# Two drains of TensorE in each group of four tiles of a graph layer

## The chip, the cores and the metric

The kernel runs on one core of a Trainium2 chip. Its time is the device time of one execution, in microseconds. A core has five engines with an instruction queue each: TensorE (PE; its weight loads are listed apart as PEld), VectorE (DVE), ScalarE (ACT), GpSimd (POOL) and SyncE (SP), which here issues transfers. Engines wait for each other through semaphores.

## The reference, cut to what matters

The reference is one layer of a graph network over 12500 nodes and 400000 edges with 128 features. Edges are sorted by `dst`; `src` is random. With `smu` a smooth bend (a linear part plus a Gelu-like part):

```
h   = max(layernorm(x), 0) @ W_in2f.T
Wij = (smu(edge_attr_20 @ W_f1.T + b_f1) @ W_f2.T + b_f2) * edge_weight[:, None]
agg = segment_sum(h[dst] * Wij, src, num_segments=12500)
out = x + smu(agg @ W_o1.T + b_o1) @ W_o2.T + b_o2
```

## The kernel before, in words

The 400000 edges are 3125 tiles of 128. Four tiles make a group (`GRP = 4`), two groups a super. A message of an edge is a row of 128 numbers. Since `src` is random, rows are first scattered by GpSimd into DRAM buffers, sorted by bins of 128 nodes; then the kept rows of a bin are fetched again and summed by TensorE with a one-hot matrix. The supers are cut into ten epochs (`PARTS`): while the rows of one epoch are made and scattered, the kept rows of the epoch before are summed. The first epoch has nothing to sum.

The order on TensorE, VectorE, ScalarE and SyncE is written out by hand (a manual schedule): each engine takes its instructions in the order in which the loop over `p`, the place of a group, names them. Semaphore waits are added where data or a buffer asks for them. In one turn the loop works on several groups at once. The steps, with the tile that each writes and its line:

- `turn` (L707): four transposes into `pt` on TensorE (L709, four matmuls, for the last epochs). `send` (L718 or L720, then four times L723): ScalarE scales `pt` into the message rows `ms`, and GpSimd scatters them (L738), four indirect transfers a group.
- `weigh` (L686): `pw`, an fp32 matmul of 128x512, from `sm`. `gather` (L667): `ph`, the rows of `h` by a one-hot matrix. `take` (L675): ScalarE copies `ph` into `hg`.
- `parts(...)`: sums of kept rows. It calls `add` (L799), fp32 matmuls of 128x128 into `pg`; about half of a turn's share stands here, the other half at the end of the turn. `add` also has VectorE make one-hot matrices (`se`, L783) and add a full `pg` to `agg` (L812), and has SyncE fetch the next rows (L769).
- `mix` (L696): VectorE, `mt` from `pw` and `hg`.
- `hide` (L633): `pu`, an fp32 matmul of 128x512. `bend` (L641): ScalarE, `ge` from `pu`. `smooth` (L649): VectorE, `sm` from `pu` and `ge`; the next turn's `weigh` reads it.
- `count` (L578, L580, L581): three small matmuls into `pc`, and `read` (L608), VectorE, `sl` from `pc`. `bins` (L564) and `pick_part` (L531, L532) make one-hot matrices for later groups.
- `step()`: in the first epoch, pieces of the preparation of `h` and of the indices.

`pu`, `pw`, `ph`, `pt` and `pc` have one PSUM bank each, `pg` has two. A tile is written again only when its readers are done. TensorE's order in a turn is so: `pt`, `pw`, `ph`, first half of the sums, `pu`, `pc`, second half of the sums.

```
            parts(lo + (hi - lo) // 2)
            mix(at(p + 1))
...
            read(at(p + 2))
            parts(hi)
            step()
```

Of the kernel before, what the change touches and what calls it, by code (L numbers as in the profile page):

```python
# [43 lines left out]
def gnn_kernel(  # L44
# [19 lines left out]
    nc = tc.nc  # L64
# [239 lines left out]
    with tc.tile_pool(name="ld", bufs=4) as ld, \  # L304
# [173 lines left out]
        def at(p):  # L478
            return seq[p] if p < len(seq) else NG

        def sup_at(p):
            return flow[p] if p < len(flow) else NS
# [5 lines left out]
        def load(s):  # L488
            if s >= NS:
                return  # L490
            t0, nt = sups[s]
            e0, n = t0 * P, nt * P
            fb = fbufs[place_of[s] % NF]
            if s > 0:
                nc.sync.dma_start(fb[0:R, :n], f_t[:, e0:e0 + n])
            loaded[s] = (fb,)
            if s > 2:
                targets(s)
# [112 lines left out]
        def number(g):  # L611
            if g >= NG:
                return
            (t, n), k = groups[g], epoch[g // PER]
            t0, hic = begins[k]
            if s_of(g) < EARLY:
                ix = cnt.tile([P, GRP], I32, name="ix", bufs=8)
            else:
                ix = ix_kept[:, t - kept_tile:t - kept_tile + n]
            nc.vector.scalar_tensor_tensor(ix[:, :n], slots.pop(g)[:, :n], BIG + CAP[k] - 1, hic[:, t - t0:t - t0 + n],  # L620
                                           op0=ALU.min, op1=ALU.add)
            taken[g] = ix
# [3 lines left out]
        def hide(g):  # L626

            if g >= NG:
                return
            n = groups[g][1] * P  # L630
            o = g % PER * GRP * P
            pu = ps1.tile([P, GRP * P], F32, name="pu")
            nc.tensor.matmul(pu[:, :n], w_f1, loaded[g // PER][0][:, o:o + n], start=True, stop=True)  # L633
            units_of[g] = pu
# [20 lines left out]
        def gather(g):  # L655

            if g >= NG:
                return
            n = groups[g][1] * P
            o = g % PER * GRP * P  # L660
            oh, hw = onehot[g // PER], loaded[g // PER][2]
            ph = ps1.tile([P, GRP * P], F32, name="ph")
            if g // PER < FEW // SUP:
                for q in range(3):
                    nc.tensor.matmul(ph[:, :n], hw[:, q * D:(q + 1) * D], oh[:, o:o + n], start=(q == 0), stop=(q == 2))
            else:
                nc.tensor.matmul(ph[:, :n], hw[:3 * WIN, g % PER, :], oh[:3 * WIN, o:o + n], start=True, stop=True)  # L667
            rows_of[g] = ph

        def take(g):  # L670
            if g >= NG:
                return
            n = groups[g][1] * P
            hg = edge.tile([P, GRP * P], F32, name="hg")
            nc.scalar.activation(hg[:, :n], rows_of[g][:, :n], AF.Copy)  # L675
            rows_of[g] = hg
# [3 lines left out]
        def weigh(g):  # L680

            if g >= NG:
                return
            n = groups[g][1] * P
            pw = ps1.tile([P, GRP * P], F32, name="pw")
            nc.tensor.matmul(pw[:, :n], w_f2, hidden.pop(g)[:, :n], start=True, stop=True)  # L686
            pws[g] = pw
# [3 lines left out]
        def mix(g):  # L691
            if g >= NG:
                return
            n = groups[g][1] * P
            mt = edge.tile([P, GRP * P], F32, name="mt", bufs=3)
            nc.vector.scalar_tensor_tensor(mt[:, :n], pws.pop(g)[:, :n], b2, rows_of.pop(g)[:, :n],  # L696
                                           op0=ALU.add, op1=ALU.mult)
            mixed[g] = mt

        def turn(g):  # L700

            n = groups[g][1]
            pt = ps1.tile([P, GRP, P], F32, name="pt")
            mt = mixed.pop(g)
            for j in range(n):
                if s_of(g) < EARLY:
                    nc.tensor.transpose(pt[:, j, :], mt[:, j * P:(j + 1) * P], ident)  # L707
                else:
                    nc.tensor.matmul(pt[:, j, :], mt[:, j * P:(j + 1) * P], w_o1, start=True, stop=True)  # L709
            mixed[g] = pt  # L710

        def send(g):

            t, n = groups[g]
            ms = msg.tile([P, GRP, ROW], F32, name="ms")
            m = epoch[s_of(g)] // BUFS
            if m:
                nc.scalar.activation(ms[:, :n, P], lo_b[:, t:t + n], AF.Identity, bias=mark[:, m:m + 1])  # L718
            else:
                nc.scalar.activation(ms[:, :n, P], lo_b[:, t:t + n], AF.Copy)  # L720
            pt = mixed.pop(g)
            for j in range(n):
                nc.scalar.activation(ms[:, j, 0:P], pt[:, j], AF.Copy, scale=w_sb[:, t + j:t + j + 1])  # L723
            if s_of(g) >= EARLY:
                nc.scalar.dma_start(kept_rows[:, t - kept_tile:t - kept_tile + n, :], ms[:, :n, :])
                return
            scatter(g, ms)
# [59 lines left out]
        def add(k, b, q):  # L787

            g = b % GRP
            c, i = b // SPAN[k], b % SPAN[k]  # L790
            halved = k == EPOCHS - 1 and b // GRP == whole // GRP - 1
            if halved:
                g %= GRP // 2
            if q == 0 and g == 0:
                pgs[0] = ps2.tile([P, GRP, P], F32, name="pg")
            if q == 0 and i == 0:
                choose(k, behind(k, c, 1))
            o = i * Q[k] + q
            nc.tensor.matmul(pgs[0][:, g, :], rows_in[c][:, o, 0:P], sel[c][:, o, :], start=(q == 0),  # L799
                             stop=(q == Q[k] - 1))  # L800
            if q < Q[k] - 1:
                return
            if i == SPAN[k] - 1 or b == NB - 1:
                rows_in.pop(c), sel.pop(c)
                fetch(k, behind(k, c, AHEAD))
            if g == GRP - 1 or b == NB - 1 or halved and g == GRP // 2 - 1:
                dst = agg[:, (b - g) * P:(b + 1) * P]
                src = pgs[0][:, :g + 1].rearrange("p b n -> p (b n)")
                if k == 0:
                    nc.vector.tensor_copy(dst, src)  # L810
                else:
                    nc.vector.tensor_add(dst, dst, src)  # L812
                if k == EPOCHS - SENT_LAST - 1:
                    plain.append(dst)
                    if len(plain) > 1:
                        fold()
# [20 lines left out]
        def parts(upto):  # L837
            nonlocal done
            while done < upto:
                add(summing, *work[done])  # L840
                done += 1
# [236 lines left out]
        def step():  # L1078

            nonlocal taken_steps, slot, apart_by  # L1080
            if opening:
                apart_by += 1
                if apart_by % 2 == 0:
                    opening.pop(0)()
                return
            slot += 1
            while taken_steps < COUNT and taken_steps * 3 * (eps_of[0][1] * PER - 22) < slot * COUNT:
                steps[taken_steps]()
                taken_steps += 1
# [49 lines left out]
        for p in range(len(seq)):  # L1139
            g = seq[p]  # L1140
            s = g // PER
            if p == (FEW // SUP - 3) * PER:
                assert not opening
            if p % PER == 0:
                load(sup_at(p // PER + 3))
            if s < EARLY:
                k = chores(g)
            else:
                lo = hi = done
            if p > 1 and p != SLACK:  # L1150
                turn(at(p - (p > SLACK)))
                send(at(p - (p > SLACK)))
            step()
            number(at(p + 1))
            weigh(at(p + 1))
            gather(at(p + 1))
            take(at(p + 1))
            parts(lo + (hi - lo) // 2)
            mix(at(p + 1))
            if p == 0:  # L1160
                turn(at(1))
                send(at(1))
                pick_part(at(2))
            step()
            hide(at(p + 2))
            bend(at(p + 2))
            count(at(p + 2))
            smooth(at(p + 2))
            pick_part(at(p + 3))
            bins(at(p + 3))  # L1170
            read(at(p + 2))
            parts(hi)
            step()
            assert k == 0 or taken_steps == COUNT

# [281 lines left out]
```

## Time and profile before

| | |
|---|---|
| median of 3 runs | 5191.76 us (5183.92 to 5208.39) |
| profiled execution | 5192.84 us |
| its span | 5190.7 us, 69995 instructions |
| TensorE busy | 3896.6 us (75%) |
| VectorE, ScalarE, GpSimd busy | 3349.5 (65%), 2957.4 (57%), 3042.1 us (59%) |
| mean granted clock of TensorE | 0.887 |

How to read the profile. A group's row gives the source line, engine, operation, what is written and read, the count, then the busy time in us, the mean of one in ns, the idle time of the engine just before, and what ended most of that. The chain of waits is followed back from the last instruction, at each step to what released it, or to the instruction before it on its engine; "issue" in it is time in which the engine waited for nothing that the profile shows. In a list of waits stand the waiter, what ended the wait, the total in us, the number of times and the longest. In a timeline stand start and duration in us, with the idle time before in brackets. The ends of matmuls are modelled: they say when the last result should be out, and the next matmul may start before that. In the source view of a line the durations are in ns, as least, median and greatest.

### The profile page before, as it was taken

Reading aid. Unit: us, or ns where it says so; the run is one execution under the profiler, and the core shown is the slowest. Engines: PE = TensorE matmul, PEld = TensorE weight load, DVE = VectorE, ACT = ScalarE, POOL = GpSimd, SP = SyncE. Lnnn points to the kernel's source line nnn. Section 1 sums busy time; section 2 is a strip of 40 time slices with the busy share of each in tenths; the row PEclk is TensorE's granted clock in tenths of the full one; section 3 lists DMA queues with packets and bytes.
Section 4 is the critical chain, followed back from the end, with each engine's and each line's share of the span. In section 5 each row is a group of like instructions: output and inputs, shape, how many; then the busy total and the mean of one; then the engine's idle time right before and its main releaser. Section 6 shows DMA issues by size and latency. Waiting matters only on the chain.

```text
span 5190.7 us, 69995 instructions
## 1 busy us (share of the span) xinstructions
PE 3896.6 (75%) x18475; PEld 2442.9 (47%) x18475; DVE 3349.5 (65%) x7364; ACT 2957.4 (57%) x7286; POOL 3042.1 (59%) x3170
## 2 busy tenths in 40 slices
PE   7667767777777777777777777777778877777456
PEld 3233334444444444444444444545455555545446
DVE  6675656666666666666666666666667767667236
ACT  6567866666565565666566666655556655555001
POOL 5666665555555555555565555555656665555554
PEclk9888888988898989989898989999989999989678
DMA  5644434544444443343444344444444444444566
GB/s 158 169 138 139 141 112 147 145 146 145 139 133 122 117 118 116 118 119 115 116 125 117 118 118 131 128 129 127 124 131 145 143 128 147 140 122 147 191 195 199
DMA packets 509824, 708.03 MB, mean 136 GB/s; under 512 B 174382, under 2 KB 362815, under 8 KB 509289
## 3 DMA queue, kind: packets, MB, share of 16 engines
q1 hardware_dynamic: 401992, 484.14, 33.2%
q0 software_dynamic: 100112, 207.06, 12.1%
q10 hardware_dynamic: 7312, 12.29, 0.6%
q8 instruction: 147, 2.41, 0.2%
q14 instruction: 261, 2.13, 0.2%
HBM read 409.48 MB, written 293.71 MB: 135 GB/s over the span
## 4 chain that ended last, share of the span: by engine, by line
PE 49%; DVE 17%; ACT 12%; issue 11%; another core or an unknown queue 10%; DMA 1%; ACTq 0%; POOL 0%; DVEq 0%; POOLq 0%
PE pw L686 14%; PE pg L799 13%; PE pu L633 10%; ACT ms L723 5%; DVE mt L696 5%; DVE sm L649 4%; PE ph L667 3%; DVE se L783 3%; PE pt L707 3%; ACT hg L675 3%; ACT ge L641 2%; DVE so L564 2%; PE pc L581 1%; PE pc L578 1%
## 5 line engine op out<-in xcount | busy, mean ns | idle before, releaser
L738 POOL DMA_INDIRECT buf<-ms,ix x2944 | 2826.0, 960 | 1974.5 <-ACT ms L723 1196.9
L686 PE MATMUL pw<-sm,w_f 128*128 128x512 f32 x1562 | 1024.6, 742 | 771.9 <-DVE sm L649 479.1
L799 PEld LDWEIGHTS pg<-se,rw 128*128 128x128 f32 x8036 | 1153.0, 207 | 450.6 <-issue 372.6
L799 PE MATMUL pg<-se,rw 128*128 128x128 f32 x8036 | 1245.6, 295 | 134.1 <-issue 101.3
L723 ACT ACTIVATE ms<-pt,w_sb 128x128 f32<-128x128 f32 x3121 | 879.5, 363 | 816.5 <-PE pc L581 294.4
L696 DVE SCALAR_TENSOR_TENSOR mt<-pw,b,hg 128x512 f32<-128x512 f32 x781 | 584.0, 748 | 790.5 <-ACT hg L675 585.8
L564 DVE SCALAR_TENSOR_TENSOR so<-irow_ps,hi_f,so 128x98 f16<-128x98 f32 x2936 | 931.4, 317 | 80.3 <-DVE so L564 2.3
L633 PE MATMUL pu<-f,w_f 128*128 128x512 f32 x1562 | 904.6, 664 | 0.0
L641 ACT ACTIVATE ge<-pu 128x512 f32<-128x512 f32 x781 | 472.2, 605 | 740.3 <-remote 224.0
L649 DVE SCALAR_TENSOR_TENSOR sm<-pu,ge 128x512 f32<-128x512 f32 x781 | 535.0, 685 | 477.0 <-ACT ge L641 269.3
L686 PEld LDWEIGHTS pw<-sm,w_f 128*128 128x128 f32 x1562 | 261.2, 210 | 926.6 <-DVE sm L649 553.0
L707 PE MATMUL pt<-ident,mt 128*128 128x128 f32 x2940 | 468.0, 283 | 266.6 <-ACT ms L723 208.7
L675 ACT ACTIVATE hg<-ph 128x512 f32<-128x512 f32 x781 | 472.6, 605 | 289.5 <-PE ph L667 85.2
L783 DVE TENSOR_TENSOR se<-irow_ps,rw 128x1536 f32<-128x1536 f32 (+1 forms) x345 | 587.9, 1704 | 71.9 <-remote 28.3
L532 ACT ACTIVATE oh<-oh,onesb 128x512 bf16<-128x512 bf16 x780 | 562.6, 721 | 26.2 <-ACT oh L531 0.9
L531 ACT ACTIVATE oh<-rbc,nrow 128x512 bf16<-128x512 uint8 x762 | 553.3, 726 | 0.0
L707 PEld LDWEIGHTS pt<-ident,mt 128*128 128x128 f32 x2940 | 341.8, 145 | 312.9 <-ACT ms L723 243.2
L608 DVE TENSOR_REDUCE sl<-pc 128x4 f32<-128x392 f32 x782 | 435.5, 557 | 67.1 <-PE ph L667 22.9
L667 PE MATMUL ph<-oh,hw 126*128 126x512 bf16 x762 | 337.7, 443 | 0.0
L633 PEld LDWEIGHTS pu<-f,w_f 128*128 128x128 f32 x1562 | 292.2, 221 | 81.3 <-issue 66.1
L812 DVE TENSOR_TENSOR agg<-agg,pg 128x512 f32<-128x512 f32 (+1 forms) x200 | 134.4, 672 | 281.2 <-remote 178.1
L578 PE MATMUL pc<-so,tri 128*128 128x392 f16 x736 | 254.4, 346 | 20.6 <-DVE sl L608 13.6
(218 smaller groups left out, 2120.6 us busy)
## 6 DMA issues: line engine op xcount, KB each, us to landing
rw<-buf SPq DMA_DIRECT2D x292, 774.0 KB
buf<-zero SPq DMA_DIRECT2D x146, 387.0 KB
rbc<-rel_dram SPq DMA_DIRECT2D x389, 128.0 KB
buf<-ms,ix POOLq DMA_INDIRECT x2944
rw<-buf SPq DMA_DIRECT2D x49, 645.0 KB
f<-in_f_t SPq DMA_DIRECT2D x390, 80.0 KB
hw<-h_dram SPq DMA_DIRECT2D x762, 31.5 KB
kept_rows<-ms ACTq DMA_DIRECT2D x45, 258.0 KB
```

The source lines that it names most:

```text
L564: nc.vector.scalar_tensor_tensor(so[:, j], irow_ps[:, :NB], hi_f[:, t + j:t + j + 1], so[:, j - 1] if j else before, op0=ALU.is_equal, op1 ...
L633: nc.tensor.matmul(pu[:, :n], w_f1, loaded[g // PER][0][:, o:o + n], start=True, stop=True)
L641: nc.scalar.activation(ge[:, :n], units_of[g][:, :n], AF.Gelu, scale=ZS)
L649: nc.vector.scalar_tensor_tensor(sm[:, :n], units_of.pop(g)[:, :n], LIN, hidden[g][:, :n], op0=ALU.mult, op1=ALU.add)
L675: nc.scalar.activation(hg[:, :n], rows_of[g][:, :n], AF.Copy)
L686: nc.tensor.matmul(pw[:, :n], w_f2, hidden.pop(g)[:, :n], start=True, stop=True)
L696: nc.vector.scalar_tensor_tensor(mt[:, :n], pws.pop(g)[:, :n], b2, rows_of.pop(g)[:, :n], op0=ALU.add, op1=ALU.mult)
L707: nc.tensor.transpose(pt[:, j, :], mt[:, j * P:(j + 1) * P], ident)
L723: nc.scalar.activation(ms[:, j, 0:P], pt[:, j], AF.Copy, scale=w_sb[:, t + j:t + j + 1])
L738: i = nc.gpsimd.indirect_dma_start(out=bufs[k][:, :], out_offset=bass.IndirectOffsetOnAxis(ap=ix[:, j:j + 1], axis=0), in_=ms[:, j, :], in ...
L783: nc.vector.tensor_tensor(se[:, a:a + n], own.unsqueeze(1).to_broadcast([P, n, P]), rows_in[c][:, a:a + n, P:P + 1].to_broadcast([P, n, P] ...
L799: nc.tensor.matmul(pgs[0][:, g, :], rows_in[c][:, o, 0:P], sel[c][:, o, :], start=(q == 0), stop=(q == Q[k] - 1))
```

## The change

A call is added in two places of the loop. It puts a drain instruction into TensorE's queue, which is to hold back what follows on TensorE until what stands ahead of it there is done. The first stands behind the first half of the sums (`mix` in between is VectorE's), ahead of `hide`. The second stands behind the second half of the sums, ahead of the next turn's `turn` and `weigh`. There are 782 turns, so 1564 drains. Nothing else in the order of any engine is changed.

```
--- before.py
+++ after.py
@@ -1157,6 +1157,7 @@
             take(at(p + 1))
             parts(lo + (hi - lo) // 2)
             mix(at(p + 1))
+            nc.tensor.drain()
             if p == 0:
                 turn(at(1))
                 send(at(1))
@@ -1170,6 +1171,7 @@
             bins(at(p + 3))
             read(at(p + 2))
             parts(hi)
+            nc.tensor.drain()
             step()
             assert k == 0 or taken_steps == COUNT
 
```

More of the change, by code (lines that the diff above doesn't have):

```diff
@@ L1159, in gnn_kernel @@
             mix(at(p + 1))
+            nc.tensor.drain()
             if p == 0:
@@ L1172, in gnn_kernel @@
             parts(hi)
+            nc.tensor.drain()
             step()
```

## The prediction

> **What bounds the kernel now.** I read the page first, then the chain of waits, then the waits of TensorE, then a timeline of some groups. The page gives the span, TensorE's busy share and the chain by engine; the chain's own view gives finer shares by line.
>
> ```profile
> span 5190.7 us, 69995 instructions
> PE 49%; DVE 17%; ACT 12%; issue 11%; another core or an unknown queue 10%; DMA 1%; ACTq 0%; POOL 0%; DVEq 0%; POOLq 0%
> L686 PE MATMUL pw<-sm,w_f 128*128 128x512 f32 x1562 | 1024.6, 742 | 771.9 <-DVE sm L649 479.1
> ...
> L633 PE MATMUL pu<-f,w_f 128*128 128x512 f32 x1562 | 904.6, 664 | 0.0
> ```
> ```profile
> core 0: 5190.7 us, clock 0.887
> ```
> ```profile
> by line: PE pw L686 14.3%; PE pg L799 12.9%; issue 11.4%; another core or an unknown queue 9.6%; PE pu L633 9.6%; ACT ms L723 4.8%; DVE mt L696 4.6%; DVE sm L649 3.9%; PE ph L667 3.4%; DVE se L783 3.1%; PE pt L707 2.7%; ACT hg L675 2.5%; AC
> ```
>
> Half of the chain runs through TensorE, but no engine is full: `pw` alone sees 771.9 us of idle TensorE before it. An fp32 matmul leaves two records, so x1562 is 781 groups of four tiles, some 6 us each; the 782 turns of the loop hold 1564 drains. How the chain goes through a group shows in the chain between 2404 and 2413 us:
>
> ```profile
> 2404.44 2.68 issue
> 2407.12 1.12 PE pw L686 x2
> 2408.24 0.22 PE ph L667
> 2408.46 0.45 PE pg L799 x4
> 2408.91 0.86 PE pu L633 x2
> ...
> 2410.11 0.74 PE pg L799 x6
> 2410.84 0.44 PE pt L707 x4
> 2411.28 0.49 issue
> 2411.77 1.14 PE pw L686 x2
> ```
>
> Reader: one turn of TensorE, from `pw` over the first half of the sums (`pg`), `pu`, the second half, `pt`, back to `pw`, is 4.16 us of work (2407.12 to 2411.28) in 4.65 us. The first drain stands between the first `pg` and `pu`, the second between the second `pg` and `pt`. While the chain runs on TensorE its pieces follow each other without a hole, since a matmul starts before the one ahead has ended. Where TensorE waits, it is nearly always at these two places:
>
> ```profile
> PE pw L686 <- DVE sm L649: 479.1, 269, 7.8
> PE pt L707 <- ACT ms L723: 208.7, 147, 3.5
> PE pw L686 <- issue: 182.8, 152, 5.5
> ...
> PE pw L686 <- DVE mt L696: 81.7, 73, 2.6
> ...
> PE pt L707 <- DVE mt L696: 32.4, 13, 8.4
> ...
> PE pt L707 <- issue: 20.8, 18, 6.3
> ```
>
> So `pw` waits in 494 of 781 groups, and the true loop is `pu` -> ScalarE's `ge` -> VectorE's `sm` -> the next `pw`. `pu` lies on that loop; `pt` mostly does not.
>
> **What one drain costs.** Nothing is removed or moved; each drain adds a wait, for TensorE's own earlier work. Queued behind the first are `pu`, the three counts `pc` and the second half of the sums; ScalarE's `ge` and VectorE's `sl` wait for these. Queued behind the second are `pt`, `pw` and `ph`; ScalarE's `ms` and `hg` and VectorE's `mt` wait for them, and SyncE's fetch of the next rows for the sums. In the first part of the run there are no sums yet, and the drains stand behind `ph` and `pc`.
>
> The trace has no drain behind matmuls, so the price comes from both sides. The cheap end is the drain records themselves, at the program's end:
>
> ```profile
> L1453 POOLq DRAIN  x3: 40/113/4402, 5180.7 to 5190.4; - x3
> ...
> L1453 PEldq DRAIN  x2: 8/8/8, 5187.9 to 5190.2; - x2
> ```
>
> TensorE's took 8 ns with nothing ahead of them, and one of GpSimd's stood 4402 ns, so a drain can stand long. The other end is a restart after a wait, next to a matmul in the stream:
>
> ```profile
> 2416.39 0.69 DVE L649 SCALAR_TENSOR_TENSOR sm<-pu,ge 128x512 f32<-128x512 f32 x1
> 2417.13 1.12 PE L686 MATMUL pw<-sm,w_f 128*128 128x512 f32 x2 [1.20 <-DVE mt L696]
> 2418.09 0.38 PE L667 MATMUL ph<-oh,hw 126*128 126x512 bf16 x1
> 2418.75 1.02 PE L633 MATMUL pu<-f,w_f 128*128 128x512 f32 x2
> ```
>
> `sm` ends at 2417.08 and `pw` starts at 2417.13: 0.05 to 0.06 us of restart. From idle the pair takes 1.12 us on the chain, in the stream an equal pair (`pu`) advances it by 0.86: 0.26 us, since its weights are then loaded in the open and the overlap with the matmul ahead (`pw` ends at 2418.25, `ph` starts at 2418.09) is gone. I take 0.26 + 0.06 = 0.32 us for a drain that waits for the array, because a drain makes exactly the state that `pw` starts from.
>
> The Trainium skill, PSUM — Partial Sum Buffer, section Engine vs sequencer instructions, says that a drain waits for the engine to go fully idle; by that the 8 ns are no price, and GpSimd's 4402 ns agrees. Its page TensorE: Matmul & The Clock Gate, section Single matmul latency, puts the part of a matmul that is hidden in a stream at 398 cycles of 2.4 GHz, an estimate of 0.17 us a drain; the trace shows an overlap of 0.16 us, and by that alone the sum below would be about half.
>
> **The sum.** First drain: `pu` has 9.6% of the span on the chain, 498 us. One pass is 0.86 us at full clock, 0.97 at the mean clock of 0.887, so some 514 groups have it on the chain: 514 x 0.32 = 164 us. In the other groups `ge` is held by something later and the drain is hidden. Second drain: in the 494 groups in which `pw` waits, `pw` still comes when `sm` does, and the drain vanishes there. Of the 287 others, `pt` itself already waits in 178 of 781 groups (23%), for ScalarE, and a drain costs nothing beside that wait: 222 groups x 0.32 = 71 us. I take half, 35 us, by judgement: in the chain above `pt` is followed both times by an issue piece, not by `pw`. Together 199 us. The profiled execution took 5192.84 us (span 5190.7 and 2.1 around it), the median of the runs is 5191.76; so **5192.84 + 199 = 5392 us**. Own range of this case: 5275 (0.16 us, the lost overlap alone, at the 514 first drains) to 5520 (both drains on the path in two groups of three, 781 x 2/3 x 0.64 = 333 us).
>
> **Rivals.** One thing in the trace makes a drain's price uncertain: signals of TensorE that arrive late.
>
> ```profile
> 2415.33 0.60 PE L707 MATMUL pt<-ident,mt 128*128 128x128 f32 x4
> ...
> 2416.32 0.29 ACT L718 ACTIVATE ms<-lo_b,mark 128x4 f32<-128x4 bf16 x1
> ...
> 2420.86 1.14 ACT L723 ACTIVATE ms<-pt,w_sb 128x128 f32<-128x128 f32 x4 [4.25 <-PE pc L581]
> ...
> 2422.35 0.62 ACT L641 ACTIVATE ge<-pu 128x512 f32<-128x512 f32 x1
> ...
> 2423.92 0.70 PE L686 MATMUL pw<-sm,w_f 128*128 128x512 f32 x1 [1.21 <-DVE mt L696]
> ```
> ```profile
>   PE pc L581: 294.4, 92
>   remote: 241.4, 68
>   PE pg L799: 120.3, 39
>   PE pu L633: 76.0, 32
>   PE ph L667: 66.7, 44
>   PE pt L707: 6.9, 13
> ```
>
> `ms` reads only `pt`, which ended at 2415.93, yet starts 4.9 us later. By the source view of L723 (second fence) this is common: 798.8 us of ScalarE's idle time in 275 cases, 2.9 us each, end at other matmuls' signals or at none that is known, and only 6.9 us at `pt`. Something holds TensorE's signals back while its matmuls go on.
>
> 1. *The drain waits for held signals too* (slower still). Then TensorE, which now runs ahead during a hold, stands to its end. In the case shown this would be free: with `pu` restarted at 2420.9 it ends by 2422.0, before `ge` at 2422.35, and the rest, 0.34 of counts (2409.77 to 2410.11 in the chain above), 0.74 of sums, 0.32 and 0.44 of `pt`, by 2423.9, when `pw` starts at 2423.92. It costs where a held signal has no reader waiting; no view counts those. With half as many as the seen ones, 138, at 2.9 us less the mean idle before `pw` (771.9 / 781 = 1.0 us), it is 262 us more: 5654; with as many, 5915. For it: 4402 ns of GpSimd's drain.
> 2. *Faster.* If a full TensorE queue is what holds the signals, emptying it twice a group lets `ms`, and so `hg` and `mt`, go sooner. With half of the 798.8 us taken as on the path, it wins if more than 199 / 400, one half, of the holds go; with three quarters gone, 5192.84 + 199 - 300 = 5092. Against it: holds outlast an idle TensorE, as here, where TensorE had stood idle for 2.1 of its 3.31 us when the late `ms` began:
>
> ```profile
> 2432.19 1.14 ACT L723 ACTIVATE ms<-pt,w_sb 128x128 f32<-128x128 f32 x4 [3.88 <-remote]
> 2433.39 2.08 PE L709 MATMUL pt<-w_o,mt 128*128 128x128 f32 x8 [3.31 <-ACT ms L723]
> ```
>
> 3. *The drain does nothing*: it only passes TensorE's sequencer, at 8 ns. 1564 x 0.008 = 12.5 us, all on the path: 5205, no change that can be told.
>
> **How the numbers follow.** The runs before lie within 0.5% of each other, so 0.5% (26 us) is about what can be told from no change. Forecast as summed: 0.43. Held signals: 0.34. No effect: 0.10. Faster: 0.13. So faster 0.13, same 0.10, slower 0.77. The range reaches down to 5150, which leaves out about two thirds of the faster case (0.09), and up to 5780, which leaves out the upper third of the held-signal case (0.10). The likeliest case alone is 5275 to 5520.
>
> **What would show it.** Right: `pu` loses its overlap with the sums, its idle time before rises from 0 to 0.2 us or more in nearly every group, and its mean grows from 664 ns towards the 742 of `pw`; `pt` gains idle time that is put down to no engine; `pw` waits less. Held signals: drain records on TensorE of 1 us and more, and `pu` idle by over 1 us a group. Faster: ScalarE's idle time before L723 falls by more than half. No effect: `pu` still starts before the last `pg` ends (its idle time before is 0.0 us in its row above). My forecast is wrong if the time is under 5218 us, or if `pu`'s idle time is there and the span does not grow by half of it.

## The result, and the profile after

The changed kernel takes 5917.48 us (median of 6 runs, 5893.33 to 5975.86), the kernel before 5210.66 us in the same set (6 runs, 5183.92 to 5230.16). The ratio is 1.1374, with an interval of 1.1314 to 1.1434: slower, and beyond the predicted range, which ended at 5780. It lies 2.5 us from the upper figure of the first rival, "with as many, 5915". The profiled execution took 5923.98 us, 731 more than that of before.

For what follows one thing must be known: the kernel before took about 5200 us in some sets of runs and 4037 us in others, each set on one chip and steady in itself, so every difference in time below is taken inside its own set, unless it is said that two sets are compared.

The page of the changed kernel: the span, TensorE's busy time, the chain by engine, and the groups of `pu`, `ge`, `pw` and `pt` (busy us, mean ns | idle us before).

```profile
span 5921.8 us, 71559 instructions
...
PE 4258.6 (72%) x18475; PEld 2605.8 (44%) x18475; DVE 3367.3 (57%) x7364; ACT 2999.2 (51%) x7286; POOL 3041.4 (51%) x3170
...
PE 60%; issue 25%; ACT 7%; DVE 4%; another core or an unknown queue 3%; DMA 1%; SPq 0%; ACTq 0%; DVEq 0%
...
L633 PE MATMUL pu<-f,w_f 128*128 128x512 f32 x1562 | 1062.1, 767 | 1004.7 <-issue 949.3
...
L641 ACT ACTIVATE ge<-pu 128x512 f32<-128x512 f32 x781 | 466.9, 598 | 1709.7 <-PE pu L633 1365.5
...
L686 PE MATMUL pw<-sm,w_f 128*128 128x512 f32 x1562 | 907.4, 665 | 71.0 <-DVE sm L649 39.4
...
L707 PE MATMUL pt<-ident,mt 128*128 128x128 f32 x2940 | 541.3, 313 | 305.8 <-issue 221.0
```

The idle time of TensorE has changed places: `pu` had 0.0 and has 1004.7 us, `pw` had 771.9 and has 71.0. In all TensorE is busy for 362 us more (4258.6 against 3896.6) and idle for 369 us more (5921.8 - 4258.6 = 1663.2, against 5190.7 - 3896.6 = 1294.1); together 731, the whole difference. In the chain, "issue", waits for nothing that the profile shows, grew from 11% to 25%.

The waits of TensorE in the changed kernel (waiter, what ended the wait, us in total, times, longest):

```profile
PE pu L633 <- issue: 949.3, 273, 8.1
PE pt L707 <- issue: 221.0, 95, 5.6
...
PE pt L709 <- issue: 43.4, 12, 5.0
PE pw L686 <- DVE sm L649: 39.4, 54, 2.6
```

These are not 781 small restarts but 273 + 95 + 12 = 380 long stops, 1213.7 us in all, 3.2 us each on the mean, nearly all of them behind the two drains (`pt` had 18 waits of this kind before, 20.8 us). The source views of the drains themselves and of L723 (durations in ns as least, median, greatest; then who ended ScalarE's idle time, in us and times):

```profile
L1160 PEldq DRAIN  x782: 593/2651/9807, 17.2 to 5525.9; - x196
```
```profile
L1174 PEldq DRAIN  x782: 1157/2373/7612, 20.5 to 5527.8; - x196
```
```profile
  PE pt L707: 383.0, 282
...
  remote: 30.4, 11
```

Before, `ms` (L723) waited for signals that were named after matmuls behind `pt` (294.4 us at `pc`, 241.4 unknown, 120.3 at `pg`), and 6.9 us at `pt`. Now it is `pt` itself, since TensorE can no longer run ahead of a late signal. The timeline shows one such stop, at the second drain (start, duration, idle before in brackets):

```profile
2697.45 0.21 PE L581 MATMUL pc<-so,rest_h 128*128 128x98 f16 x1
...
2701.93 0.57 DVE L608 TENSOR_REDUCE sl<-pc 128x4 f32<-128x392 f32 x1 [1.70 <-remote]
...
2702.66 2.07 PE L709 MATMUL pt<-w_o,mt 128*128 128x128 f32 x8 [5.00 <-issue]
2704.52 1.91 PE L686 MATMUL pw<-sm,w_f 128*128 128x512 f32 x2
...
2708.79 1.15 PE L709 MATMUL pt<-w_o,mt 128*128 128x128 f32 x8
...
2709.78 1.10 PE L686 MATMUL pw<-sm,w_f 128*128 128x512 f32 x2
```

The last count ends at 2697.66, and TensorE has nothing in flight. VectorE's `sl`, which reads that count, starts only at 2701.93, 4.3 us later. The drain lets `pt` go at 2702.66, 5.0 us after the array's last work. So the drain did not wait for the array; it let go only after the late signal had gone out.

One stop is one case. The trace also records the updates of semaphores, which are the signals themselves. It has 393 idle times of TensorE of over 0.5 us that end with a drain. In 277 of them a signal of TensorE goes out more than 0.15 us after the array fell idle, and from the last such signal to TensorE's next matmul it is 0.14 us at the median. (In the others none is recorded, but about a quarter of TensorE's updates are missing from this trace; the last section comes back to this.) In the trace of the same kernel without late signals (both_again, below) none of TensorE's 106 idle times of that length ends with a drain, and none has a signal inside. That the drain waits for the signals is the plain reading; that both wait for a third thing, these records do not exclude.

There is a second bill: `pt` then takes 2.07 us where the next one takes 1.15, and `pw` 1.91 where the next takes 1.10. The windows behind the stop and one turn later (us, busy time of the engines, then the granted clock) say why:

```profile
2702.70:2708.20 5.50, 5.39 (x14) 2.92 (x15) 0.68 (x1) 1.74 (x5) 0.00 (x0) 0.56 0.13 49
2708.70:2713.00 4.30, 4.10 (x21) 2.65 (x21) 2.80 (x8) 3.61 (x10) 0.00 (x0) 1.00 0.12 16
```

The granted clock is 0.56 in the 5.5 us behind the stop and 1.00 after that. The Trainium skill, TensorE: Matmul & The Clock Gate, section What's actually happening, has the array fall to half its clock after an idle window of about 3.4 us and come back after a busy one of the same length. The trace's records of the clock put the half from 2700.70 to 2707.53 us: the fall, 3.0 us after the last count's end, agrees, while the full clock came back 4.9 us after TensorE had started again, later than that.

A turn without a late signal shows the plain price of a drain, in the chain of the changed kernel:

```profile
2711.55 0.11 issue
2711.66 1.12 PE pu L633 x2
...
2713.85 0.08 issue
2713.93 0.65 PE pt L707 x4
```

`pu` costs 0.11 + 1.12 where it cost 0.86, so 0.37 us; `pt` 0.08 + 0.65 where it cost 0.44, so 0.29 us. The predicted 0.32 lies between them.

### The profile page after: what moved, and what is told of

The parts are those of the page before. It is cut to its first block, busy times and chain, and to the rows that moved or that the text cites. A ratio compares the mean times of both kernels' runs of the same rounds, so it can differ in the third digit from the quotient of the medians.

```text
span 5921.8 us, 71559 instructions
## 1 busy us (share of the span) xinstructions
PE 4258.6 (72%) x18475; PEld 2605.8 (44%) x18475; DVE 3367.3 (57%) x7364; ACT 2999.2 (51%) x7286; POOL 3041.4 (51%) x3170
## 4 chain that ended last, share of the span: by engine, by line
PE 60%; issue 25%; ACT 7%; DVE 4%; another core or an unknown queue 3%; DMA 1%; SPq 0%; ACTq 0%; DVEq 0%
PE pg L799 16%; PE pu L633 16%; PE pw L686 12%; PE pt L707 8%; PE ph L667 3%; PE pc L578 2%; ACT ge L641 2%; ACT oh L531 2%; PE pc L580 1%; ACT ms L723 1%; DVE se L783 1%; PE pt L709 1%; DVE sm L649 1%; DVE mt L696 1%
## 5 line engine op out<-in xcount | busy, mean ns | idle before, releaser
L738 POOL DMA_INDIRECT buf<-ms,ix x2944 | 2825.4, 960 | 2705.0 <-ACT ms L723 1908.4
L633 PE MATMUL pu<-f,w_f 128*128 128x512 f32 x1562 | 1062.1, 767 | 1004.7 <-issue 949.3
L799 PE MATMUL pg<-se,rw 128*128 128x128 f32 x8036 | 1325.6, 309 | 101.3 <-issue 83.3
L799 PEld LDWEIGHTS pg<-se,rw 128*128 128x128 f32 x8036 | 1221.4, 219 | 384.9 <-issue 315.8
L723 ACT ACTIVATE ms<-pt,w_sb 128x128 f32<-128x128 f32 x3121 | 881.0, 364 | 529.0 <-PE pt L707 383.0
L686 PE MATMUL pw<-sm,w_f 128*128 128x512 f32 x1562 | 907.4, 665 | 71.0 <-DVE sm L649 39.4
L633 PEld LDWEIGHTS pu<-f,w_f 128*128 128x128 f32 x1562 | 274.1, 220 | 1257.5 <-issue 1236.4
L707 PE MATMUL pt<-ident,mt 128*128 128x128 f32 x2940 | 541.3, 313 | 305.8 <-issue 221.0
L667 PE MATMUL ph<-oh,hw 126*128 126x512 bf16 x762 | 311.0, 408 | 0.0
L578 PE MATMUL pc<-so,tri 128*128 128x392 f16 x736 | 280.3, 381 | 0.2 <-DVE so L564 0.2
```

Source lines behind the costliest of these rows:

```text
L738: i = nc.gpsimd.indirect_dma_start(out=bufs[k][:, :], out_offset=bass.IndirectOffsetOnAxis(ap=ix[:, j:j + 1], axis=0), in_=ms[:, j, :], in ...
```

## The experiments

Two theories were to be told apart. **H**: a drain waits for signals of TensorE that come late, and the 707 us (5917.48 - 5210.66) are mostly those stops. **R**: the drains cost their restarts, 0.3 us each where they lie on the path, and nothing else. The kernel before was run beside all of them. Times are medians in us, each beside the median of the kernel before in the same set:

| kernel | drains | before | time | difference | ratio |
|---|---|---|---|---|---|
| d1_only | first place alone | 4037.09 | 4080.31 | +43 | 1.0107 (1.009 to 1.0123) |
| d2_only | second place alone | 4037.09 | 4035.53 | -2 | 0.9999 (0.999 to 1.0009) |
| ns_before | none, no scatter | 4037.09 | 3807.61 | -229 | 0.9433 (0.9418 to 0.9449) |
| ns_after | both, no scatter | 4037.09 | 3995.14 | -42 | 0.9898 (0.9882 to 0.9915) |
| both_again | both | 4035.28 | 4100.21 | +65 | 1.016 (1.0143 to 1.0177) |
| four_each | four at each place | 4035.28 | 4350.15 | +315 | 1.0782 (1.0764 to 1.08) |
| both_third | both | 4036.34 | 4101.47 | +65 | 1.0161 (1.014 to 1.0181) |
| ns_after2 | both, no scatter | 4036.34 | 3994.25 | -42 | 0.9895 (0.9875 to 0.9915) |
| drain_at_pw | one, between `pt` and `pw` | 4036.34 | 4037.11 | +1 | 1.0002 (0.9992 to 1.0011) |
| ahead_of_sums | both, each ahead of its half of the sums | 4044.78 | 4116.24 | +71 | 1.0177 (1.016 to 1.0194) |
| ns_before2 | none, no scatter | 4044.78 | 3806.21 | -239 | 0.941 (0.9391 to 0.9429) |
| first_epoch | both, first epoch only | 5288.05 | 5307.20 | +19 | 1.0039 (1.0002 to 1.0076) |
| both_hold | both | 5179.48 | 5928.63 | +749 | 1.1444 (1.136 to 1.1528) |
| d1_hold | first place alone | 5179.48 | 5615.51 | +436 | 1.084 (1.0759 to 1.0921) |
| d2_hold | second place alone | 5179.48 | 5473.99 | +295 | 1.0563 (1.0486 to 1.064) |
| pw_hold | one, between `pt` and `pw` | 5179.48 | 5413.26 | +234 | 1.0429 (1.0337 to 1.0521) |

before_again (the kernel before, 4036.85) and ns_after3 (no scatter, both drains, 3996.98, beside a kernel before of 5288.05) have one time each and no interval.

**One place at a time, d1_only and d2_only.** Each keeps one of the two calls:

```
             mix(at(p + 1))
+            nc.tensor.drain()        (d1_only)
...
             parts(hi)
+            nc.tensor.drain()        (d2_only)
```

> Only the first drain of each turn is kept (behind the first half of the sums, ahead of pu). Theory H (a drain waits until TensorE's signals are out, and these are held back for microseconds at a time): a hold is met by whichever drain comes first in it, so one drain alone meets most holds and the two single costs sum to more than the 727 us of both: here 450 to 600 us over before, about 5650 to 5800, and idle time before pu of 800 to 1000 us. Theory R (a drain costs its restart, and nothing else): the chain of the changed kernel gives 1.23 us for drain, restart and pu in place of 0.86, so 0.37 x 782 = 289 us at most, and the costs of the two add up to the whole.

> Only the second drain of each turn is kept (behind the second half of the sums, ahead of pt). Theory H: 300 to 500 us over before, about 5500 to 5700, with idle time before pt well above the 266.6 us of before, and this plus the first drain's own cost above 727 us. Theory R: 0.29 x 782 = 227 us at most, and it adds up with the first to 727 us or less.

The first drain alone cost 43 us and the second nothing. But the kernel before stood at 4037 us here, not 5200, so neither theory was tested by this set: whatever is late in the result's profile was not there.

**Without the scatter, ns_before and ns_after.** GpSimd's scatter (L738) returns before it issues, and the buffers are cleared whole, so kept rows are sums of zeros; TensorE, VectorE and ScalarE keep their instructions.

```
-    CB = 2
+    CB = 1
...
+                return               (ahead of L738)
```

> The kernel before with GpSimd's indirect transfers of the message rows (L738) left out; the buffers are cleared whole in their place, so that the sums read zeros. The output is not the reference's. Theory H, with the scatter as what holds TensorE's signals: the idle time of ScalarE before L723 that ends at other matmuls' signals than pt's falls from 799 us to under 150, and the time falls to 4000 to 4500 us. If the scatter does not hold them, that idle time stays above 500 us.

> The changed kernel with the scatter left out in the same way; the output is not the reference's. Theory H with the scatter as the holder: both drains cost their restart alone, at most 0.37 + 0.29 us a turn, 516 us, and less where TensorE waits anyway: 150 to 450 us over the same kernel without drains, and no drain record much above 4 us. Theory R: the same 600 to 800 us as with the scatter, or more, since TensorE then sets the pace alone. If the holds have another cause, the long drains (up to 9.8 us) stay.

Nothing was late in this set even with the scatter, so the pair does not yet tell whether the scatter holds the signals; the 4000 to 4500 us expected of ns_before were missed for the same reason. The pair does give a price of restarts: the drains cost 3995.14 - 3807.61 = 188 us here, near the 199 of the prediction's sum. The pages say where that holds, in ns_before and in ns_after:

```profile
PE 3421.0 (90%) x18470; PEld 2229.7 (59%) x18475; DVE 3318.4 (87%) x7364; ACT 2955.7 (78%) x7286; POOL 41.4 (1%) x45
```
```profile
PE 3684.7 (92%) x18470; PEld 2265.5 (57%) x18475; DVE 3333.7 (84%) x7364; ACT 2948.6 (74%) x7286; POOL 41.4 (1%) x45
```

TensorE is busy for 90% of that span, and the scatter, whose transfers make most of the 14% that DMA holds in the chain of the kernel before at this speed (before_again, below), is gone. It fits that fewer restarts find cover then; no run varies this alone. ns_after2 and ns_before2 repeat the pair in two other sets and give the same times within 2 us.

> The changed kernel without the scatter (part of the computation is left out), once more. If before takes about 4037 us: 3995 as before. If before takes some 5200 us: theory H with the scatter as the holder says under 4300 us and no drain above 6 us; if something else holds the signals, the time stays above 4600 us.

> The kernel before without the scatter (part of the computation is left out), once more. If before takes about 4037 us: 3808 again. If it takes some 5200 us: the scatter as the holder says under 4200 us, and ScalarE's idle time before L723 under 150 us; something else as the holder says over 4600 us.

**The changed kernel and the kernel before again, both_again and before_again.** Both are unchanged copies.

> The changed kernel once more, beside a kernel before that may take 4037 us, as in the last set, or some 5200, as in the first. Theory H (the 727 us come from TensorE's signals held back): where before takes about 4037 us and ScalarE's idle time before L723 ends at pt alone, both drains cost about their two single costs, 43 and 0 us, and at most the 188 us that they cost without the scatter: 4080 to 4220 us. Where before takes about 5200, the ratio is 1.13 again. Theory R (restart, whatever the signals do): 1.10 to 1.14 in both.

> The kernel before, for its profile in this set. Theory H: if it takes about 4037 us, the list of what ends ScalarE's idle time before L723 holds pt alone (under 20 us in all, in place of 799 us at other signals), and SyncE's register moves (L519, up to 1395 ns in the first set) all take under 60 ns; if it takes about 5200, both are as in the first set. Rival: the 1150 us between the sets are the granted clock or the transfers alone, and the odd idle time before L723 is in both.

This set too had its kernel before at 4035 us, and the change cost 65 us. before_again shows what is missing at that speed: in the source view of L723 nothing is late, in that of SyncE's L519 no register instruction is long, and `pw` waits 423 times.

```profile
  PE pt L707: 8.7, 9
  PE pt L709: 0.2, 1
```
```profile
L519 SPq MOVE hw<-h_dram x762: 29/38/39, 81.3 to 3678.9; - x191
```
```profile
PE pw L686 <- DVE sm L649: 357.4, 423, 3.4
```

In the trace of before that the prediction was made from, the same row of L519 reaches 1395 ns:

```profile
L519 SPq MOVE hw<-h_dram x762: 2/38/1395, 95.6 to 4754.1; - x191
```

So the late signals (some 800 us of ScalarE's idle time at L723) do not come from the program alone: the same kernel has 8.9 us here. The page of before_again, and that of both_again with the row of `pu`:

```profile
PE 3478.3 (86%) x18475; PEld 2257.8 (56%) x18475; DVE 3325.1 (82%) x7364; ACT 2952.7 (73%) x7286; POOL 3041.5 (75%) x3170
...
PE 34%; DVE 31%; DMA 14%; ACT 11%; issue 5%; POOL 4%; ACTq 0%; DVEq 0%; SPq 0%; POOLq 0%
```
```profile
PE 3707.9 (90%) x18475; PEld 2279.0 (56%) x18475; DVE 3339.7 (81%) x7364; ACT 2947.0 (72%) x7286; POOL 3043.5 (74%) x3170
...
PE 61%; DVE 15%; ACT 8%; DMA 6%; issue 6%; POOL 3%; ACTq 0%; DVEq 0%; SPq 0%; POOLq 0%
...
L633 PE MATMUL pu<-f,w_f 128*128 128x512 f32 x1562 | 885.3, 649 | 74.3 <-issue 0.2
```

The wait of `pw` in both_again:

```profile
PE pw L686 <- DVE sm L649: 114.0, 180, 2.8
```

`pu` idles for 74.3 us, 0.1 us a group, with no long stop. `pw`'s wait for `sm` fell by 243 us, so most of the restarts came out of time in which TensorE had waited anyway. The chain agrees: TensorE's share rose from 34% to 61%, while VectorE's fell from 31% to 15% and that of transfers from 14% to 6%; where those set the pace before, a restart had cover. both_third repeats it (+65 again) on another chip.

> The changed kernel, to see which of the two conditions this set has. If before takes about 4037 us: 4100, ratio 1.016, by every theory now. If before takes some 5200 us: theory H says ratio 1.12 to 1.15.

**Four drains in a row at each place, four_each.**

```
+            for _ in range(4):
+                nc.tensor.drain()    (at both places)
```

> Four drains in a row in place of each one. If a drain costs the emptying and the restart once, and nothing as an instruction, the three others cost 8 to 60 ns each where TensorE sets the pace: 0 to 100 us over both_again. If each is a step of TensorE's sequencer as long as those that SyncE showed in the first set (some 700 ns), it is over 1000 us.

4350.15 - 4100.21 = 250 us for 3 x 1564 = 4692 more drains, 53 ns each, and more than the 0 to 100 us expected. A drain behind a drain is no restart, but its price is not the 13 ns (the median) of its record either:

```profile
L1161 PEldq DRAIN  x3128: 7/13/5390, 16.9 to 4048.4; - x196
```

**Other places, drain_at_pw and ahead_of_sums.** One drain a turn just ahead of `weigh`; and both drains, each ahead of its half of the sums instead of behind it.

```
             step()
+            nc.tensor.drain()        (drain_at_pw)
             number(at(p + 1))
             weigh(at(p + 1))
...
+            nc.tensor.drain()        (ahead_of_sums)
             parts(lo + (hi - lo) // 2)
...
+            nc.tensor.drain()        (ahead_of_sums)
             parts(hi)
```

> One drain a turn, between pt and pw, where TensorE waits for sm anyway in 423 of the 781 groups of before at 4035 us. If a drain costs only where TensorE would have gone on, this one costs least of the three places: 0 to 30 us over before (the first place cost 43, the second nothing). If its price is paid wherever it stands, 60 us or more (0.1 us x 781 and the lost overlap).

> Both drains moved ahead of their half of the sums: behind ph, and behind pc. Theory: the price is the restart wherever TensorE would have gone on, so where before takes 4037 us it is the same 40 to 90 us as behind the sums; rival: it is the load of an fp32 operand of 512 columns (pu) in the open that costs, and ahead of the sums (128 columns) it is under 25 us. Where before takes some 5200 us, theory H says 500 to 900 us in either place.

Ahead of `pw`, where TensorE waits for `sm` in half of the groups, a drain costs 1 us in all; ahead of the sums the pair costs 71 us. Without late signals the price depends on the place. It is not the 512 columns of `pu` that cost, since ahead of the 128 columns of the sums the pair costs no less.

**The first epoch alone, and without the scatter once more, first_epoch and ns_after3.** Both drains under `if k == 0`, so 118 turns of 782.

> Both drains in the turns of the first epoch alone (118 of 782 turns), in which no sums are made and they stand behind ph and pc. Theory: TensorE has spare time there (busy 7 to 8 tenths against 9 later where before takes 4037 us), so they cost under 5 us there; by even shares of the 64 us it would be 10 us. Where before takes some 5200 us, theory H, with holds in every stage, says 118/782 of 727 us, 80 to 140 us.

> The changed kernel without the scatter (part of the computation is left out). Where before takes about 4037 us: 3995 as before. Where it takes some 5200 us: the scatter as the holder says under 4300 us, another holder over 4600 us.

This set had its kernel before at 5288 us, with late signals. ns_after3 still took 3996.98 us, within 3 us of the sets without them, and its L723 and L519 are quiet:

```profile
  PE pt L707: 8.9, 8
```
```profile
L519 SPq MOVE hw<-h_dram x762: 29/38/39, 85.7 to 3747.5; - x191
```

So the signals are late only with the scatter in the kernel, on an occasion on which the kernel with the scatter has them. This rests on one run. Leaving the scatter out also takes away its records in the trace, which matters below. first_epoch missed: +19 us, hardly clear of noise (ratio 1.0002 to 1.0076), where H had 80 to 140. The waits of TensorE in the first 800 us, of before (from the first set) and of first_epoch, suggest why:

```profile
PE pw L686 <- DVE sm L649: 94.3, 40, 7.8
PE pw L686 <- issue: 34.9, 33, 5.5
...
PE pt L707 <- issue: 18.0, 14, 6.3
```
```profile
PE pu L633 <- issue: 57.6, 18, 7.7
PE pw L686 <- DVE sm L649: 31.7, 34, 2.6
...
PE pt L707 <- issue: 19.4, 16, 4.7
PE pw L686 <- issue: 16.4, 29, 1.7
```

The first drain stops `pu` for 57.6 us, while `pt` waits without a named cause about as long as before (19.4 us and 18.0), and `pw`'s waits fall from 129.2 to 48.1: there the stops mostly take the place of another wait. There are at most 18 + 16 = 34 stops in 118 turns, against 380 in 782. What one turn loses in the first epoch is no measure for the others.

**One place at a time where signals are late, both_hold, d1_hold, d2_hold and pw_hold.** The edits are those of both_again, d1_only, d2_only and drain_at_pw.

> The changed kernel once more, to set the two places against it in one set of runs. Theory H (a drain also waits for signals of TensorE that come late): where the kernel before stands near 5200 and ScalarE's L723 shows some 800 us of idle time put to other matmuls than pt, the ratio is 1.12 to 1.15, +650 to +750 us. Theory R (restarts alone): +65 us as in the sets where the kernel before stood at 4037, ratio 1.012. Where it stands at 4037 again both give +65.

> Only the first drain, ahead of pu. Theory H, with the kernel before near 5200: this one carries more of the loss, since 254 of the 365 long drains stood at it: by counts 254 / 365 of 707 = 490 us, ratio 1.09. Theory R: +43 us, as measured with the kernel before at 4037. If the kernel before stands at 4037: +43 by both.

> Only the second drain, ahead of pt and pw. Theory H, with the kernel before near 5200: 111 / 365 of 707 = 215 us, ratio 1.04; if one drain a turn catches what the other would have caught, this one alone costs more than its share, up to 490. Theory R: 0, as measured with the kernel before at 4037. If the kernel before stands at 4037: 0 by both.

> One drain a turn between pt and pw. Theory H, with the kernel before near 5200: a signal of pt that is held stops pw, which it did not before, so 150 to 500 us slower, with L1153 drain records of 3 us and more. Theory R: 0, as measured with the kernel before at 4037.

The kernel before stood at 5179 us, and now the theories could be told apart. H holds: +436 and +295 us for edits that cost +43 and -2 us without late signals, and +234 us for the drain ahead of `pw`, which had cost 1 us. R alone gives none of these. The two places add: 436 + 295 = 731, against 749 for both. By counts H had expected 490 and 215; its first form, written for d1_only, had the two single costs sum to clearly more than both, and that did not happen. The longest waits of TensorE, in both_hold, d1_hold, d2_hold and pw_hold:

```profile
PE pu L633 <- issue: 938.6, 272, 7.8
PE pt L707 <- issue: 212.4, 92, 5.2
```
```profile
PE pu L633 <- issue: 1043.0, 357, 8.1
```
```profile
PE pt L707 <- issue: 746.1, 218, 8.6
```
```profile
PE pw L686 <- DVE sm L649: 508.5, 191, 6.1
PE pw L686 <- issue: 334.8, 165, 9.4
```

Alone, each drain has more long stops (357 at `pu`, 218 at `pt`) than in the pair (272 and 92). That fits a late signal that stops TensorE at whichever drain comes next. Yet the times add, so a stop's length is not its cost: in d2_hold 746.1 us of stops cost 295 us. How much of a stop takes the place of another wait was not measured by place.

## Why the prediction was wrong

**The price of a drain** that meets no late signal was right: 0.32 us taken, 0.37 at `pu` and 0.29 at `pt`, in one turn of the trace.

**The restarts' sum** was too large. "514 x 0.32 = 164 us" for the first drain measured 43 us, "I take half, 35 us" for the second measured 0, and both together 65 us instead of 199, though in sets whose kernel before is faster. The step that failed is the count of groups from a share of the chain: a piece on the chain stops being the bound as soon as it grows by more than the lead of what comes next, here `pw`'s wait for `sm`, which gave up 243 us. What the restarts alone cost in a set with late signals was not measured. A sum of that size, 188 us, was paid only without the scatter.

**The choice between the cases** was the error that decided. The forecast's sum put the wait for late signals at nothing and left it to a rival. The signs asked for of that rival were there: `pu` idles for 1004.7 / 781 = 1.3 us a group ("over 1 us a group") and there are drains of up to 9.8 us. The signs of the forecast itself came too (the mean of `pu` rose to 767 ns, and `pw` waits less), so they did not tell the two apart. Within the rival the step that failed is "With half as many as the seen ones, 138": no row stood behind the half, and the one case followed by hand came out free. There were 380 stops of 3.2 us on the mean; 275 cases of 2.9 us had been seen at L723. A late signal stops a drain whether or not a reader waits for it, so the seen cases were too low a count, not too high a one. That the figure 5915 lies 2.5 us from the time is luck: it holds 199 us of restarts and 523 for late signals, while the runs give 65 and 749 - 65 = 684, the difference taken across two sets. The lower clock behind a stop was in neither. Of the 362 us that TensorE is busy longer, 230 are there without late signals too (3707.9 in both_again, 3478.3 in before_again); the other 132 fit the lower mean clock, 0.848 against 0.887, though again across sets.

**One sign was badly chosen.** "Drain records on TensorE of 1 us and more" does not tell the cases apart: without late signals the medians are nearly as long. TensorE idles before `pu` for only 0.1 us a group there, so most of a record runs while the matmuls ahead still work. In both_again:

```profile
L1160 PEldq DRAIN  x782: 592/1925/5390, 16.9 to 3793.1; - x196
```
```profile
L1174 PEldq DRAIN  x782: 760/2163/3622, 20.3 to 3794.7; - x196
```

Only the idle time of the instruction behind the drain does.

**The other rivals** fell. Emptying TensorE's queue did not make anything faster where signals are late: both_hold, d1_hold, d2_hold and pw_hold are all slower, and ScalarE's idle time before L723 fell from 816.5 to 529.0 us, not by half. And the drains do something, since `pu` idles behind them without late signals too (74.3 us in both_again, 0.0 in the kernel before).

**The range** ended at 5780 by cutting "the upper third of the held-signal case", whose upper figure was the only one with a count from the trace behind it. (The 5520 of the likeliest case alone should be 5526 by its own sum, 5192.84 + 333.)

## What to carry to other kernels

Before a wait is added to an engine, look for readers that start long after their input is done: if `ms` waits 4.9 us for a matmul that ended, its producer's signals are late, and an instruction that waits for completion may wait as long, as the drain did here, with a slow stretch after it. Cost a restart by the engine's spare time, not by its share of the chain, which gives way to the next branch. And compare only inside one set of runs: the kernel before alone differed by 1150 us between sets.

## What of the hardware was unexpected

With the scatter's transfers in the kernel, completion signals of TensorE came late (2.9 us on the mean at L723, 4.3 in the stop shown above) in three sets of runs (the first one, and those on chips 2 and 8), and SyncE's register instructions, 38 ns as a rule, took up to 1397 ns (d1_hold) in these traces. Only TensorE's signals are late in the trace of before: of the waits of `ms` (over 0.15 us), 280 of 298 last over 0.5 us beyond the end of the last `pt` matmul, while none of 329 waits of `sm` lasts so long beyond the end of ScalarE's `ge`, and one of 505 waits of `pw` beyond that of VectorE's `sm`. In four sets, on chips 1, 4 (twice) and 6, the same program with the same data showed neither, and took 4035 to 4045 instead of 5180 to 5290 us. Without the scatter it showed neither in any set. What makes the difference between the chips or the moments, and which part of the scatter holds the signals up, the runs do not settle.

One rival was not tested: the recording itself. Every time on record comes with a span and a granted clock, so the profiler was recording in all of them. In the traces with late signals most records of semaphore updates are missing: before has 31492 of them and before_again, the same kernel, 93501, with 69995 instructions in both. All seven traces with late signals have 31492 to 38024 of them, the eight others with the scatter 92947 to 93501; the five without the scatter have 44174 or 44175, since fewer are made. So the signals were late exactly where the recording lost them, and whether they are late when nothing records is not shown. It also means that the names behind a wait ("PE pc", "remote", "issue") are unsure in the traces with late signals; the starts and durations do not rest on these records.

A drain waits for such a signal too. The Trainium skill, PSUM — Partial Sum Buffer, section Engine vs sequencer instructions, says that a drain waits for the engine to go fully idle; in the stop shown above TensorE started again 5.0 us after the last matmul had ended, so "idle" here seems to include the signals that are still to go out.
